# Four graph-attention layers on one core: gather every source tile but the first by index list

## The chip, the cores and the metric

The kernel runs on one core of a Trainium2 chip. The metric is the device time of one execution in microseconds, from the first to the last instruction of the program on that core. Of the engines, PE is TensorE, DVE is VectorE, ACT is ScalarE, POOL is GpSimd and SP is the sync engine, which issues most plain transfers.

## The reference

4096 nodes with 256 features pass through four attention layers. All layers use the same 4096 x 4096 adjacency matrix, which is random and sparse: the chance of an edge between i and j falls with both indices, so low-numbered nodes have many neighbours and high-numbered ones few. Cut to what matters:

```
for each layer:
    h = relu(layernorm(x))
    g = h @ W;  e = leaky_relu(src(g)[:, None] + dst(g)[None, :], 0.2)
    x = x + act(softmax(where(adj > 0, e, -inf), axis=1) @ g)
```

Layer 0 has a bias, layer 1 an ELU at its end, layer 2 four heads of 64 features. Layer 3 takes two softmaxes, one of e and one of -e, each multiplied with a projected part of 256 features, and an ELU.

## The kernel before

Nodes are cut into NT = 32 tiles of P = 128. A unit of work computes the outputs of some target tiles; it takes its sources one step at a time. In a step, DVE makes a block of unnormalised weights `s_p` out of the target's row exponentials `s_grow`, the source's scalars and the 0/1 mask (line 1019; in layer 2 ACT makes two of the four heads, line 1005, and DVE masks them, line 1028). PE then multiplies the block with the source's features and accumulates in PSUM (`s_acc`, line 1055, for layers 0, 1 and 3; `s_accm`, line 1080, for layer 2). A column of the product holds the softmax denominator.

There are two kinds of unit. A **dense unit** serves four target tiles, a block of IB = 512 columns, and steps through all 32 source tiles. Dense units serve the first 4, 2, 1 and 1 blocks of layers 0 to 3 (`DENSE`). In layers 1 to 3 their features and masks stream from DRAM in chunks of CH = 4 tiles, `s_gs` and `s_ms`, through three buffers each; in layer 0 they lie in SBUF.

A **listed unit** serves one target tile T. Here the source rows that have any edge to the tile's 128 targets are found once, in layer 0, and packed. `CAPS[T]` is the number of groups of 128 rows that the list may fill. The features of each group are fetched by an indirect DMA from the layer's `table` in DRAM (`s_gg`, line 1215, issued by POOL, nine buffers), and the mask bytes of those rows by another into `mlist` (line 915). For target blocks 1, 2 and 3 the mask bytes ride along with a feature row once (`MASKS_IN`), and ACT copies them out into `mlist` (line 1227).

The first DP = 4 source tiles are not listed. Since nearly every row there has an edge to any tile, a listed unit takes them whole, from `pre` (`g` in layer 0) and `mpre`, which stay in SBUF. So a listed unit has 4 + `CAPS[T]` steps. In layers 1 to 3 the dense units take these four tiles from SBUF too.

Lists are made in `list_sources` for each block of four target tiles, over the JT = NT - DP tiles that are listed. A reduction over the mask marks which rows are used (`seen`, line 1316), prefix sums give each row its place, and one-hot matrices `first` (line 878) and `val` (lines 865 and 869) are multiplied on PE (`idx_ps`, line 887, one matmul per source tile) to give the row numbers `idx`.

The order of work is written out by hand in a plan of steps. In layer 0, one or two listed steps follow every dense step from step 40 on (`LISTED0`), and the chunks of the adjacency matrix of blocks 4 to 7 are loaded and turned into masks on the side. In layers 1 to 3 some dense steps run alone, and the rest are spread over the listed tiles: two per tile in layer 1, 48 over 28 tiles in layer 3. A step's gather is issued six steps ahead of its matmul. Two side queues, `posts` (layer ends and the projection for the next layer) and `lists_q`, advance by a fixed number of items per step; `gather_masks` advances by `rates[2]` gathers after every dense step of layer 0. Gathers of layers 1 to 3 need the whole layer's `table`.

The order of tiles in layer 1 is 16 to 31, then 8 to 15; in layers 2 and 3 it is 8 to 31, then 4 to 7.

Of the kernel before, what the change touches and what calls it, by code (L numbers as in the profile page):

```python
# [9 lines left out]
F16 = mybir.dt.float16  # L10
U8 = mybir.dt.uint8
I32 = mybir.dt.int32
# [5 lines left out]
P = 128  # L18
N = 4096
D = 256  # L20
NT = N // P
# [431 lines left out]

DP = CH
JT = NT - DP
TS0 = IT
DENSE = (4, 2, 1, 1)

ORDER = (None, (0, 4, 1, 5, 2, 6, 3, 7), (0, 4, 5, 6, 7, 2, 1, 3), (0, 2, 3, 4, 5, 6, 7, 1))
LISTED0 = 40
CAPS = (25, 17, 15, 13, 12, 11, 11, 10, 10, 9, 9, 9, 8, 8, 8, 8) + (8,) + (7,) * 7 + (6,) * 8
MAXCAP = max(CAPS[TS0:])
OFFS = [sum(CAPS[TS0:T]) for T in range(NT + 1)]
NLIST = OFFS[NT]
# [13 lines left out]
def list_layers(ctx: ExitStack, tc: tile.TileContext, a: dict, out: bass.AP, flag):  # L480
# [305 lines left out]

    def list_constants(pool):

        place = pool.tile([P, P, JT // 2], F16, name="place")
        nc.gpsimd.iota(  # L790
            place, pattern=[[1, P], [0, JT // 2]], base=0, channel_multiplier=0, allow_small_or_imprecise_dtypes=True
        )
        lists = pool.tile([P, MAXCAP, JT * IT], F16, name="lists")
        nc.gpsimd.iota(
            lists,
            pattern=[[1, MAXCAP], [0, JT * IT]],
            base=0,
            channel_multiplier=0,
            allow_small_or_imprecise_dtypes=True,
        )  # L800

        code = pool.tile([P, JT * IT], F16, name="code")
        n = (NT // 2 - DP) * IT
        for part, tiles, base in ((code[:, 0:n], NT // 2 - DP, DP * P - HALF), (code[:, n:], NT // 2, 1)):
            nc.gpsimd.iota(
                part,
                pattern=[[CH * P, tiles // CH], [1, CH], [0, IT]],
                base=base,
                channel_multiplier=CH,
                allow_small_or_imprecise_dtypes=True,  # L810
            )
        sums = []
        for k in range(2):
            t = pool.tile([P, NT // 2 + JT, IT], F32, name=f"sums_{k}")
            nc.gpsimd.memset(t[:, 0 : NT // 2, :], 0.0)
            sums.append(t)
        return place, lists, code, sums

    def list_sources(ib, seen, pool, consts):

        n = JT * IT
        place, lists, code, sums = consts
        half = JT // 2
# [38 lines left out]
        nc.vector.tensor_copy(hib, low[:, 1].rearrange("p j t -> p (j t)"))  # L862
        yield
        val = pool.tile([P, MAXCAP, n], F16, name=f"val_{ib}", tag="val")
        nc.vector.tensor_tensor(
            val, lists, hib.unsqueeze(1).to_broadcast([P, MAXCAP, n]), op=ALU.is_equal
        )
        yield
        nc.vector.tensor_tensor(val, val, code.unsqueeze(1).to_broadcast([P, MAXCAP, n]), op=ALU.mult)
        yield  # L870
        for t in range(IT):
            T = ib * IT + t
            cap = CAPS[T]
            ps = None
            for j in range(JT):
                if j % half == 0:
                    first = pool.tile([P, P, half], F16, name=f"first_{T}_{j}", tag="first")
                    nc.vector.tensor_tensor(  # L878
                        first,
                        place,  # L880
                        lof[:, t, j : j + half].unsqueeze(1).to_broadcast([P, P, half]),
                        op=ALU.is_equal,
                    )
                    yield
                if ps is None:
                    ps = ps_mm.tile([P, MAXCAP], F32, name=f"idx_ps_{T}", tag="mm")
                nc.tensor.matmul(  # L887
                    ps[:, 0:cap],
                    lhsT=first[:, :, j % half],
                    rhs=val[:, 0:cap, j * IT + t],  # L890
                    start=(j == 0),
                    stop=(j == JT - 1),
                )
# [284 lines left out]
    def run(plan):  # L1178

        n = len(plan)  # L1180
        for p in range(n + LEAD[3]):
# [5 lines left out]
            if p >= LEAD[3]:  # L1187
                u = plan[p - LEAD[3]][0]
                clock[0] += u.cost
                pump(posts, u.rates[0], width=2)  # L1190
                pump(lists_q, u.rates[1])
                gather_masks(u.rates[2])


    def listed_sources(L, T, pool):
# [36 lines left out]
    with ExitStack() as phase:  # L1232
# [65 lines left out]
        def mask_chunk(ib, c):  # L1298

            load()  # L1300
            if ib == 0:
                behind(c)
            m = (
                mpre[:, :, ib * IB : (ib + 1) * IB]
                if c == 0
                else mpool.tile([P, CH, IB], U8, name=f"s_m_{ib}_{c}", tag="m")
            )
            for h, raw in enumerate(loaded[ib, c]):
                nc.vector.tensor_scalar(m[:, h * half : (h + 1) * half, :], raw, 0.0, None, op0=ALU.is_gt)  # L1309
            if c > 0 or ib in MASKS_IN:  # L1310
                nc.sync.dma_start(mask_rows(ib, c * CH), m)
            if ib > 0:
                if c == 0:
                    seen[ib] = lists_p.tile([P, JT, IT], F32, name=f"seen_{ib}", tag="seen", bufs=4)
                else:
                    nc.vector.tensor_reduce(
                        seen[ib][:, (c - 1) * CH : c * CH, :].rearrange("p j t -> p (j t)"),
                        m.rearrange("p j i -> p (j i)")
                        .bitcast(I32)
                        .rearrange("p (t w) -> p t w", w=P // 4),  # L1320
                        AX.X,
                        ALU.max,
                    )
# [73 lines left out]
    for l in (1, 2, 3):  # L1397
        L = layers[l]

        def all_sources(L, T0, nt, heads, per):  # L1400


            held = {}
            n = L.part
            cols = slice(heads[0] * n, (heads[-1] + 1) * n)
            w = slice(T0 * P, (T0 + nt) * P)

            def get(i):
                jt, k = divmod(i, per)
                jt = ORDER[L.l][jt // CH] * CH + jt % CH  # L1410
                mine = heads[k : k + 1] if per > 1 else heads
                if jt < DP:
                    ensure(lambda: L.ready[jt])
                    return mine, [L.pre[:, jt, h * n : (h + 1) * n] for h in mine], mpre[:, jt, w]
                if jt % CH == 0 and k == 0:
                    ensure(lambda: all(L.ready[jt : jt + CH]))
                    gt = stream.tile(
# [112 lines left out]
```

## Time and profile before

| | |
|---|---|
| device time, median of 3 runs | 1825.72 us (1823.74 to 1826.13) |
| span of the profiled execution | 1803.2 us |
| PE busy | 1658.8 us (92%) |
| DVE busy | 1322.1 us (73%) |
| ACT busy | 634.4 us (35%) |
| POOL busy | 949.8 us (53%), of it feature gathers 748.7 us (715) and mask gathers 119.4 us (105) |
| DMA | 274.70 MB, 152 GB/s on average |
| layer 0 / 1 / 2 / 3 | 0 to 545 / 545 to 855 / 855 to 1375 / 1375 to 1803 us |

A share of busy time is a mean over stages with different limits, so it is read by stage. PE's busy time comes from records whose ends are modelled, and each float32 matmul stands in the page as two records. [...]

### The profile page before, as it was taken

The page shows a single profiled execution, that of the slowest core. Times are in us where ns is not written, and L with a number is a line of the kernel's source. Part 1 is how long each engine was busy: PE and PEld are TensorE (multiplying, and loading weights), DVE is VectorE, ACT ScalarE, POOL GpSimd, SP SyncE. Part 2 cuts the span into 40 slices and gives each one's busy share as a digit, 9 for nine tenths or more (in the row PEclk, how much of TensorE's full clock was granted, in tenths as well). Part 3 has the DMA queues.
Part 4 walks back from the last instruction along what each step waited for, and adds up shares of the span by engine and source line. Part 5 has one row for each costly group of instructions (what it writes and reads, how often), then busy time and mean ns, then how long its engine had stood idle before and what let it go on. Part 6 is the DMA issues. An engine that isn't in the chain of part 4 may idle for free.

```text
span 1803.2 us, 29164 instructions
## 1 busy us (share of the span) xinstructions
PE 1658.8 (92%) x9268; PEld 1384.2 (77%) x9268; DVE 1322.1 (73%) x3908; ACT 634.4 (35%) x1915; POOL 949.8 (53%) x930
## 2 busy tenths in 40 slices
PE   6988978889899999978999999988889999999987
PEld 5876767778778778757577777788888888888876
DVE  6877867878665667645898989887786576777755
ACT  5531012001031223233376767788894011111101
POOL 9664633745642665664165353444461666554453
PEclk9998878989989999999999999999999999999999
DMA  8888757956335444544233323333342666656554
GB/s 268 277 269 278 239 162 204 289 159 179 80 80 177 125 139 124 154 136 128 71 99 86 96 79 93 94 87 85 94 121 78 194 199 188 179 168 178 169 148 122
DMA packets 152238, 274.70 MB, mean 152 GB/s; under 512 B 21424, under 2 KB 75341, under 8 KB 152077
## 3 DMA queue, kind: packets, MB, share of 16 engines
q0 software_dynamic: 45584, 130.39, 27.1%
q1 hardware_dynamic: 105656, 141.83, 24.6%
q8 instruction: 77, 1.26, 0.3%
q14 instruction: 85, 0.69, 0.1%
q10 hardware_dynamic: 836, 0.53, 0.1%
HBM read 231.76 MB, written 40.90 MB: 151 GB/s over the span
## 4 chain that ended last, share of the span: by engine, by line
PE 71%; DVE 8%; DMA 7%; issue 5%; ACT 3%; POOL 3%; another core or an unknown queue 1%; SPq 0%; POOLq 0%; ACTq 0%; DVEq 0%
PE s_acc L1055 38%; PE s_accm L1080 21%; PE s_pj L748 6%; DMA s_raw<-in_adjT 3%; DMA s_gg<-table,idx 3%; PE idx_ps L887 2%; DVE s_p L1019 2%; PE s_sT L953 1%; PE s_tp L716 1%; DVE first L878 1%; ACT s_p L1005 1%; POOL s_z L702 1%; POOL s_gg L1215 1%; DVE s_m L1309 1%
## 5 line engine op out<-in xcount | busy, mean ns | idle before, releaser
L1215 POOL DMA_INDIRECT s_gg<-table,idx x715 | 748.7, 1047 | 764.2 <-PE s_acc L1055 298.1
L1019 DVE SCALAR_TENSOR_TENSOR s_p<-s_grow,s_gg,mlist 128x128 f32<-128x128 f32 x994 | 310.0, 348 | 140.8 <-PE s_acc L1055 70.7
L1055 PE MATMUL s_acc<-s_gg,s_p 128*128 128x257 f32 x1430 | 348.5, 387 | 8.6 <-DVE s_p L1019 6.3
L1055 PEld LDWEIGHTS s_acc<-s_gg,s_p 128*128 128x128 f32 x1430 | 269.9, 193 | 52.5 <-DVE s_p L1019 11.2
L1055 PE MATMUL s_acc<-g,s_p 128*128 128x257 f32 x1152 | 298.7, 404 | 8.0 <-DVE s_p L1019 7.7
L1055 PEld LDWEIGHTS s_acc<-g,s_p 128*128 128x128 f32 x1152 | 226.8, 203 | 42.6 <-DVE s_p L1019 10.4
L1019 DVE SCALAR_TENSOR_TENSOR s_p<-s_grow,pre,mpre 128x128 f32<-128x128 f32 (+1 forms) x576 | 190.1, 370 | 46.0 <-PE s_acc L1055 35.0
L1080 PE MATMUL s_accm<-s_p,s_gg 128*65 128x128 f32 x1744 | 204.5, 273 | 1.8 <-issue 1.8
L1055 PE MATMUL s_acc<-s_gs,s_p 128*128 128x257 f32 x896 | 205.4, 383 | 0.0
L1080 PEld LDWEIGHTS s_accm<-s_p,s_gg 128*65 128x65 f32 x1744 | 193.4, 138 | 5.3 <-issue 2.8
L1005 ACT ACTIVATE s_p<-s_grow,s_minus,s_gg 128x128 f32<-128x128 f32 x436 | 187.1, 485 | 27.1 <-PE s_accm L1080 17.8
L1019 DVE SCALAR_TENSOR_TENSOR s_p<-s_grow,s_gs,s_ms 128x512 f32<-128x512 f32 x224 | 162.3, 751 | 42.9 <-PE s_accm L1080 19.9
L1055 PE MATMUL s_acc<-pre,s_p 128*128 128x257 f32 x768 | 183.7, 383 | 7.8 <-issue 3.7
L1055 PEld LDWEIGHTS s_acc<-s_gs,s_p 128*128 128x128 f32 x896 | 170.5, 191 | 25.7 <-DVE s_p L1019 1.3
L748 PE MATMUL s_pj<-s_w,s_hT 128*128 128x259 f32 (+3 forms) x640 | 171.6, 410 | 12.7 <-ACT s_g L783 3.9
L959 ACT ACTIVATE s_grow<-s_sT 128x256 f32<-128x256 f32 (+2 forms) x136 | 46.8, 368 | 344.3 <-PE s_sT L953 227.7
L1055 PEld LDWEIGHTS s_acc<-pre,s_p 128*128 128x128 f32 x768 | 143.4, 192 | 31.3 <-issue 5.2
L748 PEld LDWEIGHTS s_pj<-s_w,s_hT 128*128 128x128 f32 x640 | 125.6, 204 | 39.5 <-issue 5.2
L915 POOL DMA_INDIRECT mlist<-mask_t,idx x105 | 119.4, 1138 | 43.1 <-issue 28.9
L1080 PE MATMUL s_accm<-s_p,pre 128*65 128x128 f32 (+1 forms) x928 | 120.5, 284 | 2.0 <-issue 1.9
L1080 PEld LDWEIGHTS s_accm<-s_p,pre 128*65 128x65 f32 x928 | 103.7, 138 | 19.3 <-issue 16.5
L1005 ACT ACTIVATE s_p<-s_grow,s_minus,pre 128x128 f32<-128x128 f32 x224 | 96.2, 487 | 19.3 <-issue 15.1
(126 smaller groups left out, 1741.8 us busy)
## 6 DMA issues: line engine op xcount, KB each, us to landing
s_raw<-in_adjT SPq DMA_DIRECT2D x128, 512.0 KB
s_gs<-table SPq DMA_DIRECT2D x28, 516.0 KB
s_gg<-table,idx POOLq DMA_INDIRECT x715
mask_t<-s_m SPq DMA_DIRECT2D x35, 256.0 KB
table<-s_g SPq DMA_DIRECT2D x28, 258.0 KB
s_ms<-mask_t SPq DMA_DIRECT2D x28, 256.0 KB
table<-s_m SPq DMA_DIRECT2D x21, 256.0 KB
table<-g SPq DMA_DIRECT2D x8, 516.0 KB
```

Source lines behind the costliest of these rows:

```text
L702: (nc.gpsimd if L.l == 0 else nc.vector).tensor_scalar(z, x[:, T, :], mv[:, k, 0:1], 0.0, op0=ALU.subtract, op1=ALU.max)
L716: nc.tensor.transpose(tp[:, c, :], zs[k][:, c * P : (c + 1) * P], ident)
L748: nc.tensor.matmul(ps, lhsT=hT[:, c, :], rhs=L.w[:, c, k * (D + 6) : k * (D + 6) + cols], start=(c == 0), stop=(c == 1),)
L878: nc.vector.tensor_tensor(first, place, lof[:, t, j : j + half].unsqueeze(1).to_broadcast([P, P, half]), op=ALU.is_equal,)
L887: nc.tensor.matmul(ps[:, 0:cap], lhsT=first[:, :, j % half], rhs=val[:, 0:cap, j * IT + t], start=(j == 0), stop=(j == JT - 1),)
L915: nc.gpsimd.indirect_dma_start(out=mlist[:, OFFS[T] + k, :], out_offset=None, in_=mask_t[T // IT], in_offset=bass.IndirectOffsetOnAxis(ap= ...
L959: nc.scalar.activation(grow[:, h1:h2, :], ps[:, h1 - h0 : h2 - h0].rearrange("p h a b -> p h (a b)"), AF.Exp, scale=scale,)
L1005: nc.scalar.activation(w[:, h, :], u.grow[:, h, :], AF.Relu, scale=g[h][:, n - 1 : n], bias=minus)
L1019: nc.vector.scalar_tensor_tensor(p[:, k, :], u.grow[:, h, :], g[k][:, n - 1 : n], m, op0=ALU.min if L.l == 3 and h == 1 else ALU.max, op1= ...
L1055: nc.tensor.matmul(u.accs[it][h], lhsT=p[:, k, it * P : (it + 1) * P], rhs=g[k][:, 0:n], start=first, stop=last,)
L1080: nc.tensor.matmul(u.regions[h], lhsT=g[k][:, 0 : DH + 1], rhs=p[:, k, :],  start=first and (u.nt > 1 or h == 0), stop=last, skip_group_ch ...
L1215: nc.gpsimd.indirect_dma_start(out=wide, out_offset=None, in_=L.table, in_offset=bass.IndirectOffsetOnAxis(ap=index[T][:, k : k + 1], axis=0),
```

## The change

DP becomes 1: only the first tile of 128 sources stays whole in SBUF, and tiles 1 to 3 are listed with the others, so that rows there without an edge to the target tile are no longer multiplied. The lists grow (`CAPS`), and JT becomes 31. Summed over the listed tiles of a layer:

| layer | listed tiles | steps before | steps after | gathers before | gathers after |
|---|---|---|---|---|---|
| 0 | 16 | 169 | 144 | 105 | 128 |
| 1 | 24 | 270 | 235 | 174 | 211 |
| 2 | 28 | 330 | 291 | 218 | 263 |
| 3 | 28 | 330 | 291 | 218 | 263 |

Mask gathers grow from 105 to 128, and ACT's copies of mask bytes from 113 to 135. The dense units of layers 1 to 3 read chunk 0 from DRAM like all others, so there are 40 loads of `s_gs` and of `s_ms` for 35. The masks of chunk 0 are written to DRAM for all eight blocks, where three were before, and seven copies put the mask of tile 0 into `mpre`. `first` takes 16 or 15 tiles at a time (`HALFT`) where it took 14. In layer 0, `gather_masks` takes five masks in four dense steps where it took four.

```diff
-DP = CH
+DP = 1
 JT = NT - DP
+HALFT = (JT + 1) // 2
...
-CAPS = (25, 17, 15, 13, 12, 11, 11, 10, 10, 9, 9, 9, 8, 8, 8, 8) + (8,) + (7,) * 7 + (6,) * 8
+CAPS = (28, 20, 17, 16, 14, 13, 13, 12, 12, 11, 11) + (10,) * 4 + (9,) * 5 + (8,) * 8 + (7,) * 4
...
-                if j % half == 0:
-                    first = pool.tile([P, P, half], F16, name=f"first_{T}_{j}", tag="first")
+                if j % HALFT == 0:
+                    n = min(HALFT, JT - j)
+                    first = pool.tile([P, P, HALFT], F16, name=f"first_{T}_{j}", tag="first")
                     nc.vector.tensor_tensor(
-                        first,
-                        place,
-                        lof[:, t, j : j + half].unsqueeze(1).to_broadcast([P, P, half]),
+                        first[:, :, 0:n],
+                        place[:, :, 0:n],
+                        lof[:, t, j : j + n].unsqueeze(1).to_broadcast([P, P, n]),
...
-                gather_masks(u.rates[2])
+                gather_masks(u.rates[2] and u.rates[2] + (plan[p - LEAD[3]][1] % 4 == 3))
...
-            m = (
-                mpre[:, :, ib * IB : (ib + 1) * IB]
-                if c == 0
-                else mpool.tile([P, CH, IB], U8, name=f"s_m_{ib}_{c}", tag="m")
-            )
+            m = mpool.tile([P, CH, IB], U8, name=f"s_m_{ib}_{c}", tag="m")
...
-            if c > 0 or ib in MASKS_IN:
-                nc.sync.dma_start(mask_rows(ib, c * CH), m)
+            nc.sync.dma_start(mask_rows(ib, c * CH), m)
...
+                    nc.scalar.copy(mpre[:, :, ib * IB : (ib + 1) * IB], m[:, 0:DP, :])
...
-                if jt < DP:
-                    ensure(lambda: L.ready[jt])
-                    return mine, [L.pre[:, jt, h * n : (h + 1) * n] for h in mine], mpre[:, jt, w]
```

More of the change, by code (lines that the diff above doesn't have):

```diff
@@ L787, in list_constants @@
     def list_constants(pool):
-        place = pool.tile([P, P, JT // 2], F16, name="place")
+        place = pool.tile([P, P, HALFT], F16, name="place")
         nc.gpsimd.iota(
-            place, pattern=[[1, P], [0, JT // 2]], base=0, channel_multiplier=0, allow_small_or_imprecise_dtypes=True
+            place, pattern=[[1, P], [0, HALFT]], base=0, channel_multiplier=0, allow_small_or_imprecise_dtypes=True
         )
@@ L802, in list_constants @@
         code = pool.tile([P, JT * IT], F16, name="code")
-        n = (NT // 2 - DP) * IT
-        for part, tiles, base in ((code[:, 0:n], NT // 2 - DP, DP * P - HALF), (code[:, n:], NT // 2, 1)):
+        n1, n2 = (CH - DP) * IT, (NT // 2 - DP) * IT
+        for part, chunks, tiles, base in (
+            (code[:, 0:n1], 1, CH - DP, DP - HALF),
+            (code[:, n1:n2], NT // 2 // CH - 1, CH, CH * P - HALF),
+            (code[:, n2:], NT // 2 // CH, CH, 1),
+        ):
             nc.gpsimd.iota(
                 part,
-                pattern=[[CH * P, tiles // CH], [1, CH], [0, IT]],
+                pattern=[[CH * P, chunks], [1, tiles], [0, IT]],
                 base=base,
@@ L822, in list_sources @@
         place, lists, code, sums = consts
-        half = JT // 2
         used = pool.tile([P, JT, IT], F16, name=f"used_{ib}", tag="used")
@@ L888, in list_sources @@
                     ps[:, 0:cap],
-                    lhsT=first[:, :, j % half],
+                    lhsT=first[:, :, j % HALFT],
                     rhs=val[:, 0:cap, j * IT + t],
@@ L1314, in mask_chunk @@
                     seen[ib] = lists_p.tile([P, JT, IT], F32, name=f"seen_{ib}", tag="seen", bufs=4)
[L1315 to L1323, printed above, removed]
+                    nc.scalar.copy(mpre[:, :, ib * IB : (ib + 1) * IB], m[:, 0:DP, :])
+                j0 = DP if c == 0 else 0
+                nc.vector.tensor_reduce(
+                    seen[ib][:, c * CH + j0 - DP : (c + 1) * CH - DP, :].rearrange("p j t -> p (j t)"),
+                    m[:, j0:, :]
+                    .rearrange("p j i -> p (j i)")
+                    .bitcast(I32)
+                    .rearrange("p (t w) -> p t w", w=P // 4),
+                    AX.X,
+                    ALU.max,
+                )
                 if c == NCH - 1:
@@ L1405, in all_sources @@
             cols = slice(heads[0] * n, (heads[-1] + 1) * n)
-            w = slice(T0 * P, (T0 + nt) * P)
             def get(i):
```

## The prediction

> **What bounds the kernel now.** I read the windows view first, cut at the layer borders, which show in the chain of waits where `s_acc` gives way to `s_accm` and back.
>
> ```profile
> core 0: us, PE busy (x) PEld busy (x) DVE busy (x) ACT busy (x) POOL busy (x), PEclk, DMA share, GB/s
> 140.00:545.00 405.00, 353.35 (x1988) 293.71 (x1987) 305.81 (x794) 54.16 (x197) 213.33 (x192) 0.89 0.62 183
> 545.00:733.00 188.00, 179.12 (x839) 150.82 (x838) 120.57 (x374) 43.66 (x154) 107.32 (x105) 0.99 0.50 142
> 733.00:855.00 122.00, 101.42 (x440) 83.70 (x439) 65.67 (x202) 38.74 (x139) 68.35 (x70) 0.92 0.48 138
> 855.00:1153.00 298.00, 296.67 (x1876) 219.49 (x1875) 266.30 (x775) 192.04 (x506) 131.76 (x119) 1.00 0.33 87
> 1153.00:1375.00 222.00, 199.73 (x1622) 185.59 (x1621) 176.97 (x624) 188.56 (x550) 100.81 (x99) 0.99 0.35 96
> 1375.00:1803.00 428.00, 411.18 (x1911) 354.95 (x1909) 280.88 (x889) 52.86 (x139) 225.63 (x218) 0.99 0.57 167
> ```
>
> The rows are: layer 0 once it has lists, layer 1 in two parts, layer 2 in two parts, layer 3. PE is full in the first part of layer 2 (296.67 of 298) and nearly so in layer 3 (411 of 428). In the second part of layer 2 nobody is full: PE 0.90, ACT 0.85, DVE 0.80, each waiting for the others. In the second part of layer 1 PE falls to 0.83.
>
> Second, the groups of instructions by line, for prices.
>
> ```profile
> L1215 POOL DMA_INDIRECT s_gg<-table,idx x715 | 748.7, 1047 | 764.2 <-PE s_acc L1055 298.1
> L1019 DVE SCALAR_TENSOR_TENSOR s_p<-s_grow,s_gg,mlist 128x128 f32<-128x128 f32 x994 | 310.0, 348 | 140.8 <-PE s_acc L1055 70.7
> L1055 PE MATMUL s_acc<-s_gg,s_p 128*128 128x257 f32 x1430 | 348.5, 387 | 8.6 <-DVE s_p L1019 6.3
> L1005 ACT ACTIVATE s_p<-s_grow,s_minus,s_gg 128x128 f32<-128x128 f32 x436 | 187.1, 485 | 27.1 <-PE s_accm L1080 17.8
> L915 POOL DMA_INDIRECT mlist<-mask_t,idx x105 | 119.4, 1138 | 43.1 <-issue 28.9
> ```
>
> Each matmul stands there as two records that overlap (1430 for 715), so its price is read from the chain, in an undisturbed run of layer 3:
>
> ```profile
> 1538.95 12.15 PE s_acc L1055 x56
> ```
>
> 56 records are 28 matmuls in 12.15 us: 0.434 us each. A listed step therefore costs PE 0.434 us in layers 0 and 1 (one matmul) and 0.868 in layer 3 (two). Layer 2 has four of half that length, 0.873 (`10.45 x84` there is 42 matmuls; with 128-wide ones alone, `2.62 x24` is 12, 0.218 each).
>
> Third, POOL's timeline in the second part of layer 1, where it gets no rest:
>
> ```profile
> 801.01 0.94 POOL L1215 DMA_INDIRECT s_gg<-table,idx  x1 [0.30 <-issue]
> 802.25 0.94 POOL L1215 DMA_INDIRECT s_gg<-table,idx  x1 [0.30 <-issue]
> 803.50 1.05 POOL L1215 DMA_INDIRECT s_gg<-table,idx  x1 [0.30 <-issue]
> 804.85 0.94 POOL L1215 DMA_INDIRECT s_gg<-table,idx  x1 [0.30 <-issue]
> ```
>
> The reader is to see the 0.30 us between gathers with nothing to wait for. Busy time leaves it out. Back to back a gather takes 1.25 us, and with the mean duration of layers 1 and 3 (1.01 and 1.035 us) 1.31 to 1.34. I use 1.31. That is more than PE's 0.868 for the step it feeds.
>
> [...]
>
> **The change, part by part.** A tile of targets has CAPS+4 sources before and CAPS+1 after. [...] So 138 steps go and 150 gathers come, with 23 more mask gathers in layer 0.
>
> Layer 2, first part (tiles 8 to 21, PE full): 19 steps fewer by 0.873 = -16.6. Second part (tiles 22 to 31 and 4 to 7): 20 fewer. A step takes ACT two activations, 2 x 0.486 = 0.97, DVE two products of 0.347 and one of 0.42 = 1.11, PE 0.873; all three are nearly full, so I take 1.05 each: -21. Against it: 8 more mask copies on ACT (0.29 each, 2.3), and POOL. A tile of 8 gathers needs 8 x 1.31 = 10.5 us there against about 12.4 of the tile (13.6 before, less one step), close enough to expose some gathers: +2. Dense chunk 0 now starts after a load: +2. Sum -31.
>
> Layer 3: 39 x 0.868 = -33.9 if PE stays the limit. Per tile PE has (c+1) x 0.868 + 0.55 for target rows + 48/28 dense steps x 1.736 = 2.98; POOL has c x 1.31. At c=7: 10.5 against 9.2; c=8: 11.3/10.5; c=9: 12.2/11.8; c=10: 13.1/13.1; c=11: 13.9/14.4; c=12: 14.8/15.7; c=13: 15.7/17.0; c=14: 16.6/18.3. The larger of each, over the 28 tiles, sums to 358 against 351 for PE alone and 385 before: -27. Nine gather buffers smooth only partly, and a tile now opens with one step from SBUF in place of four, so I give back 6: -21. DMA: 45 gathers of 264 KB in some 25 us less raises the share from 0.57 to about 0.7, below the 0.98 that layer 0 reached at 316 GB/s.
>
> Layer 1: PE per tile (c+1) x 0.434 + 3.47 (two dense steps) + 3.4 (projection of layer 2 and stalls: 310 us less 228 of matmuls over 24 tiles). Tiles 16 to 31, c 9 to 7: 11.2 to 10.3 on PE, 11.8 to 9.2 on POOL: sum 175 against 183 before, -8; I count -5. Tiles 8 to 15, c 12 to 9: POOL leads, 15.7 + 2x14.4 + 4x13.1 + 11.8 = 109 against 99 before. Measured before is 122, because ACT queues behind gathers: the copy that keeps a gathered mask (line 1227) waits for the landing, and behind it stand projection and row exponentials, for which PE waits. 14 more of these copies: I take +13. Start: the first four dense steps came from SBUF; now DVE waits for 516 KB, issued at 543.8 before and used at 550, against 546.4 for the first product: +3. Sum +11.
>
> Layer 0: PE 25 x 0.434 = -10.9, and 28 tiles x 3 more index matmuls x 0.068 (14 in 0.95 us) = +5.7. DVE -25 x 0.35, `first` 56 at 2048 or 1920 elements for 1792: +5.5 at the same rate[...]. `val` 29% larger: +3.4; seven more reductions: +3.5. POOL: 46 more by 1.35 = 62 on 213 + 190 x 0.30 = 270 of 405 us, 0.82: hidden on average, in bursts not. Five more 256 KB mask writes at 280 GB/s: 4.6 us of DMA, beside DMA-heavy work. The seven copies of tile 0's mask sit on ACT, 0.13 busy there. I take +3.
>
> Sum: +3 +11 -31 -21 = -38, so 1825.7 - 38 = 1788.
>
> **Rivals.**
> - A, POOL stays hidden. For it: POOL's average is 53% and 298 us of its waits are for PE. Then layer 0 -5, layer 1 -15, layer 2 -38, layer 3 -34: -92, 1734. Against: the 0.30 us gap, and layer 1's second part as it is.
> - B, POOL, or the landing of gathers, takes PE's place everywhere, slower than before. For it: 1.31 against 0.868. Layer 1 +30, layer 0 +25[...], layer 3 -5 if transfers slow gathers by 10%, layer 2 -22: +28, 1854. Against: dense steps, 3 us in each tile of layers 1 and 3, give POOL time to catch up.
> - C, gains and give-backs cancel: layer 3 -12, layer 2 -25, layers 0 and 1 +37: 1826.
>
> **How the numbers follow.** Forecast 0.66, A 0.12, B 0.16, C 0.06. The range reaches half way towards A and into C: 1758 to 1830. It leaves out the pure forms of A and most of B. Faster is the forecast, A and a little less where the forecast comes out poor: 0.77; same 0.05; slower 0.18.
>
> **What would show it.** In the profile after, L1215 has 865 gathers at about 1.05 us. Layer 3's span is 400 to 412 us with POOL at 0.65 to 0.7 busy; layer 2 takes about 490; layer 1 310 to 330, its second part longer than 122; layer 0 ends between 535 and 560. `first` shows 1.15 to 1.25 us[...]. The forecast is wrong if PE idles on gathers in layer 3 for more than 20 us, or if layer 2's second part loses less than 10 us.

## The result and the profile after

| | before | after |
|---|---|---|
| device time, median | 1825.93 us (1823.74 to 1833.26) | 1906.70 us (1900.23 to 1911.03) |
| ratio, 95% interval | | 1.0425 (1.0379 to 1.0471) |
| span of the profiled execution | 1803.2 us | 1898.5 us |
| mean granted PE clock | 0.963 | 0.919 |
| matmul records of PE, and their busy time | 9268, 1658.8 us | 8764, 1653.4 us |

The change makes the kernel slower by 4.2%, where 1788 us (2% faster) had been forecast.

One thing about these numbers has to be known for all that follows. The runs were made in six groups, each on one chip with the kernel before beside it. The kernel before took 1826, 1808, 1804 and 1806 us in four groups and 1727 and 1730 us in two. The ratio of the change differs with it: 1.042 in the three groups of the first kind that hold the change, 1.019 in the one of the second kind that does. I call the first kind late groups and the second prompt groups, for a reason that the last section gives. Compare ratios, and stages within one kind.

The profiled execution of the kernel before was also about 20 us shorter than the timed ones of its group. So the stages of the two profiles below differ by 95 us in sum, where the measured times differ by 81.

The windows view of the kernel after, cut at the same stages as before. Columns: time, then busy us (and instructions) of PE, weight loads, DVE, ACT and POOL, then granted clock, DMA share and GB/s.

```profile
140.00:591.00 451.00, 376.64 (x2033) 304.35 (x2031) 319.09 (x790) 55.33 (x196) 271.91 (x242) 0.82 0.60 178
591.00:806.00 215.00, 185.54 (x810) 153.38 (x811) 115.86 (x346) 43.43 (x156) 126.19 (x128) 0.92 0.49 140
806.00:941.00 135.00, 103.38 (x395) 81.17 (x394) 62.83 (x190) 43.97 (x159) 82.71 (x84) 0.85 0.49 142
941.00:1240.00 299.00, 291.03 (x1758) 207.33 (x1757) 255.74 (x732) 180.08 (x478) 157.99 (x144) 1.00 0.36 98
1240.00:1455.00 215.00, 182.56 (x1413) 171.48 (x1411) 156.87 (x544) 170.12 (x505) 117.57 (x119) 0.94 0.41 116
1455.00:1898.00 443.00, 397.90 (x1777) 331.61 (x1776) 257.92 (x819) 53.99 (x143) 261.94 (x263) 0.96 0.64 192
```

Layer 0 ends at 591 us where it was 545, layer 1 is 40 us longer (27 and 13 in its parts), layer 2 is 6 shorter and layer 3 is 15 longer. In layer 3 PE has 134 records fewer than the 1911 before and loses only 13 us of busy time, while its idle time goes from 17 to 45 us. In layer 1 it is busy 8 us longer than before with 74 records fewer: the clock column fell there from 0.99 and 0.92 to 0.92 and 0.85, and in layer 0 from 0.89 to 0.82.

The groups of instructions by line, after. The second field holds total busy time and the mean ns of one; the third is the engine's idle time before them, with what ended it.

```profile
L1220 POOL DMA_INDIRECT s_gg<-table,idx x865 | 890.6, 1030 | 679.5 <-PE s_acc L1060 173.3 <-issue 142.5 <-PE s_accm L1085 126.1
L1024 DVE SCALAR_TENSOR_TENSOR s_p<-s_grow,s_gg,mlist 128x128 f32<-128x128 f32 x1204 | 380.3, 346 | 276.9 <-DMA s_gg<-table,idx 148.5 <-PE s_acc L1060 80.6 <-PE s_accm L1085 15.9
L883 DVE TENSOR_TENSOR first<-place,lof 128x2048 f16<-128x2048 f16 x28 | 35.9, 1283 | 0.0
L883 DVE TENSOR_TENSOR first<-place,lof 128x1920 f16<-128x1920 f16 x28 | 35.4, 1263 | 45.8 <-remote 24.5 <-PE idx_ps L892 16.7 <-PE s_sT L958 3.3
```

A gather costs POOL what it cost before (a mean of 1030 ns for 1047). What changed is the second line: before the products of gathered rows DVE now sits idle for 277 us where it was 141, and for 148.5 us of it the wait ends with the landing of a gather (the end of its transfer), where it was 23.4. POOL's record of a gather ends sooner: at the median it lasts 0.947 us in the kernel before, whose chain of waits has waits of up to 5.7 us on a landing. In layer 3 alone (the view of waits, DVE, kernel before and then after; us in total, times, longest):

```profile
DVE s_p L1019 <- DMA s_gg<-table,idx: 13.2, 12, 3.0
```

```profile
DVE s_p L1024 <- DMA s_gg<-table,idx: 82.5, 72, 5.1
```

### The profile page after: what moved, and what is told of

It reads as the page before. It is cut to its first block, busy times and chain, and to the rows that moved or that the text cites. A ratio compares the mean times of both kernels' runs of the same rounds, so it can differ in the third digit from the quotient of the medians.

```text
span 1898.5 us, 28296 instructions
## 1 busy us (share of the span) xinstructions
PE 1653.4 (87%) x8764; PEld 1344.8 (71%) x8764; DVE 1272.2 (67%) x3660; ACT 612.5 (32%) x1866; POOL 1119.7 (59%) x1104
## 5 line engine op out<-in xcount | busy, mean ns | idle before, releaser
L1220 POOL DMA_INDIRECT s_gg<-table,idx x865 | 890.6, 1030 | 679.5 <-PE s_acc L1060 173.3
L1024 DVE SCALAR_TENSOR_TENSOR s_p<-s_grow,s_gg,mlist 128x128 f32<-128x128 f32 x1204 | 380.3, 346 | 276.9 <-DMA s_gg<-table,idx 148.5
L1060 PE MATMUL s_acc<-s_gg,s_p 128*128 128x257 f32 x1730 | 447.3, 403 | 29.7 <-DMA s_gg<-table,idx 11.2
L1060 PEld LDWEIGHTS s_acc<-s_gg,s_p 128*128 128x128 f32 x1730 | 341.2, 203 | 93.7 <-issue 27.4
L1085 PE MATMUL s_accm<-s_p,s_gg 128*65 128x128 f32 x2104 | 256.8, 277 | 5.8 <-issue 4.8
L1060 PEld LDWEIGHTS s_acc<-g,s_p 128*128 128x128 f32 x1056 | 215.8, 211 | 45.1 <-DVE s_p L1024 10.5
L1085 PEld LDWEIGHTS s_accm<-s_p,s_gg 128*65 128x65 f32 x2104 | 239.4, 141 | 11.7 <-issue 5.6
L1085 PE MATMUL s_accm<-s_p,s_gs 128*65 128x512 f32 x256 | 115.9, 592 | 0.0
L1024 DVE SCALAR_TENSOR_TENSOR s_p<-s_grow,g,s_m 128x512 f32<-128x512 f32 x128 | 98.0, 772 | 13.3 <-remote 5.5
L883 DVE TENSOR_TENSOR first<-place,lof 128x2048 f16<-128x2048 f16 (+1 forms) x56 | 71.3, 1273 | 45.8 <-remote 24.5
L1310 DVE TENSOR_SCALAR s_m<-s_raw 128x1024 uint8<-128x1024 int32 x128 | 90.6, 719 | 16.4 <-DMA s_raw<-in_adjT 14.1
L892 PEld LDWEIGHTS <-first 128*128 128x128 f16 x868 | 62.3, 164 | 51.9 <-DVE first L883 25.5
```

What stands on the lines that cost most here:

```text
L883: nc.vector.tensor_tensor(first[:, :, 0:n], place[:, :, 0:n], lof[:, t, j : j + n].unsqueeze(1).to_broadcast([P, P, n]), op=ALU.is_equal,)
L892: nc.tensor.matmul(ps[:, 0:cap], lhsT=first[:, :, j % HALFT], rhs=val[:, 0:cap, j * IT + t], start=(j == 0), stop=(j == JT - 1),)
L1024: nc.vector.scalar_tensor_tensor(p[:, k, :], u.grow[:, h, :], g[k][:, n - 1 : n], m, op0=ALU.min if L.l == 3 and h == 1 else ALU.max, op1= ...
L1060: nc.tensor.matmul(u.accs[it][h], lhsT=p[:, k, it * P : (it + 1) * P], rhs=g[k][:, 0:n], start=first, stop=last,)
L1085: nc.tensor.matmul(u.regions[h], lhsT=g[k][:, 0 : DH + 1], rhs=p[:, k, :],  start=first and (u.nt > 1 or h == 0), stop=last, skip_group_ch ...
L1220: nc.gpsimd.indirect_dma_start(out=wide, out_offset=None, in_=L.table, in_offset=bass.IndirectOffsetOnAxis(ap=index[T][:, k : k + 1], axis=0),
```

## The experiments

Two theories stood first. **G**: the 37 to 45 more gathers in each of layers 1 to 3 are what costs. **R**: the dense part of the change costs (the masks' new way through layer 0, and dense blocks that read chunk 0 from the table). The change was taken apart along that line.

**The dense part alone** (the lists as before, four tiles whole in SBUF):

```
- DP = 1                      + DP = CH     (lists and listed steps as before)
  CAPS = those of the kernel before
  dense blocks read chunk 0 from the table; every chunk 0 is written to HBM; ACT copies it to mpre
```

> The changed kernel with DP back at 4 and the old CAPS: steps and gathers as before, but dense units read chunk 0 from the table, chunk 0's masks are written for all blocks, and ACT copies them to mpre. If the surplus gathers cost the time (G), this part is small: within 10 us of before, 1816 to 1836. If the other parts of the change cost it (R: loads of chunk 0, ACT waiting for the mask, more DMA), most of the 81 us stays: 1865 or more.

Measured: 1755.29 us, 1.0170 (1.0132 to 1.0208), prompt group. It came out between the two theories. In two things this kernel isn't the change's dense part alone, and both lie in layer 0. Its seven copies to `mpre` hold four tiles (1.90 us each) where the change copies one (0.62 us). And it has the change's faster order of mask gathers, five in four dense steps, but only the 105 gathers of before. What came of the second is told with the chain of three kernels below.

**The shorter tiles without the surplus gathers** (the steps of the kernel after; 715 + 105 gathers instead of 865 + 128):

```
-            if i < DP:
+            if i < DP or i - DP >= CB[T]:        # CB: CAPS of the kernel before
                 the step takes tile 0 from SBUF, no gather
```

> The changed kernel, lists, steps and dense part unaltered, but in each listed unit the last CAPS(after) - CAPS(before) steps use the tile in SBUF again in place of a gathered group (their sources are left out of the sum), so that 715 feature and 105 mask gathers remain. G: PE's saving comes through, 1735 to 1785. R: the time stays near the changed kernel's, 1860 or more.

Measured: 1688.42 us, 0.9775 (0.9738 to 0.9813), prompt group, as G has it. This leaves sources out, so it isn't a usable version, but it prices the two halves of the listed part. With the surplus gathers their 22 mask copies on ACT are gone too, so the two are priced together.

**Gathers that nobody reads** (the kernel before, with the 150 more gathers, of 512 bytes a row, into two spare buffers):

```
+                if k < CA[T] - CAPS[T]:
+                    spare = pool.tile([P, 128], F32, tag="gx", bufs=2)
+                    nc.gpsimd.indirect_dma_start(out=spare, ..., index[T][:, k : k + 1])
```

> The kernel before with 150 surplus gathers (512 bytes a row, into two spare buffers that nobody reads), as many in each tile as the change adds; PE, DVE and ACT do what they did. If it is POOL's issue rate that costs the time (G1), 1850 to 1900. If it is the landing of gathers that somebody waits for (G2: data used, not issue time), at most 1845. R: at most 1835.

Measured: 1769.41 us, 1.0250 (1.0211 to 1.0289), prompt group. The group of these instructions:

```profile
L1226 POOL DMA_INDIRECT s_gx<-table,idx x150 | 155.2, 1035 | 45.7 <-issue 35.0 <-DVE s_p L1020 4.0 <-DMA s_gg<-table,idx 1.5
```

No engine computes with their data, and 0.025 x 1727 = 43 us reach the end, as a ratio within the range that was expected if issuing costs (G1). Issuing them takes 155 us of POOL plus 0.30 us between gathers. They are also issued ahead of other gathers, whose packets go through the same queue (q0 on the page of this run, 140.23 MB for 130.39 before: the 9.8 MB of the 150), and the two weren't told apart. Where the 43 us fall is read below, with the windows by layer.

**Is it the number of buffers, or the order on DVE?** With 14 gather buffers for nine, and with DVE's products three steps before the matmul turned into one (`LEAD` (0, 2, 3, 6) to (0, 2, 5, 6)), so that the reciprocals that end a tile no longer stand behind products of the next tile's gathers. Both beside a fresh run of the kernel after. The two unaltered kernels were meant for the chip of the first experiments, but this group ran on another and is a late one.

> The kernel before, unaltered, for a profile from the chip of the experiments, where the kernel before took 1727 us and not 1826. Either theory: ratio 1.00; its layers should be shorter than in the first profile, the same work in less time.

> The changed kernel, unaltered, on the chip of the experiments. G (surplus gathers cost the time) and R (the other parts): the ratio is again 1.03 to 1.05, 1780 to 1815. If the ratio is nearer to 1.00 here, the loss is of a kind that depends on the chip's memory or clock, which would speak for waits on landings.

> The changed kernel with 14 gather buffers in layers 1 to 3 in place of 9. If gathers start too late for want of buffers (G2), PE's waits shrink and layers 1 and 3 lose 10 us or more each against the changed kernel. If POOL's issue rate binds (G1), nothing starts earlier: within 5 us of the changed kernel.

> The changed kernel with weights made one step ahead of the matmul and not three (LEAD 0, 2, 5, 6). With three, the products of the next tile's first gathers stand on DVE's queue ahead of the reciprocal that frees the last tile's accumulators (H). If H costs much, layer 3 loses 10 us or more against the changed kernel, its waits of PE for s_y go, and layer 1 does not gain more than 5. If G1 alone, no gain, and a loss where PE now waits for DVE.

Measured: the kernel before 0.999 (0.994 to 1.004), after 1.0417 (1.0372 to 1.0462), 14 buffers 1.0521 (1.0459 to 1.0582), the other lead 1.0604 (1.053 to 1.0679). Neither is a cure. With 14 buffers every layer of the profile is longer than in the kernel after of this group, so want of buffers isn't the main cause. The other lead is less clear: its layer 3 took 439 us where the kernel after took 446, short of the 10 us that were expected, and its loss lies in layer 2 (522 for 510) and in layer 0 (585 for 567, within the scatter given below). It also takes away the slack of two steps, so it doesn't price the queue of reciprocals alone, and that queue isn't refuted as part of the cause.

**Bytes, PE work, the ACT copy.** Again beside the kernel after; this group was a prompt one.

```
half rows:    out=wide[:, 0 : L.part] if L.l == 3 else wide          # layer 3, both heads use head 0's columns
SBUF steps:   DP + 3 + CAPS[T] steps in layers 1 to 3, the 3 from tile 0 in SBUF
DVE copy:     nc.vector.tensor_copy(mpre[...], m[:, 0:DP, :])        # was nc.scalar.copy, line 1315
```

> The changed kernel as it is, as the yardstick for the runs beside it. Chips differ (the kernel before took 1726.9, 1808.5 and 1825.9 us on three of them), and the run with fewer gathers was made on the fastest. If the loss is in the kernel alone, the ratio to the kernel before is 1.035 to 1.05 again. If part of it comes from the chip (on the two slower ones PE's semaphore updates come late, in batches), the ratio is nearer 1.02 on a chip where they do not.

> Leaves out: in layer 3 each gather fetches only the 258 columns of head 0 (half the bytes, same number of gathers), and both heads use them. If the bytes or the landing of a gather set layer 3's pace, layer 3 falls from 443 us by 20 us or more. If what counts is the number of gathers, each 1.25 us of POOL plus its waits, layer 3 stays within 8 us of the changed kernel beside it, and so does the total.

> Adds work that counts twice: in layers 1 to 3 every listed tile opens with three more steps from the SBUF tile (84 steps a layer: 36 us of PE in layer 1, 73 in layer 2, 73 in layer 3 at full clock), as the kernel before had them; the gathers stay. If gathers set the pace of layers 1 and 3, these steps fill time in which PE waited: layer 1 grows by 0 to 12 us, layer 3 by 0 to 15, layer 2 (PE full) by 55 to 75. If PE work plus fixed waits make up the time, layer 1 grows by 36 and layer 3 by 65 to 75.

> The copy of the first tile's mask (line 1315, seven of them in layer 0) runs on DVE in place of ACT. ACT waited 26.8 us there for the mask that DVE writes, up to 12.7 at once, with row exponentials and projection queued behind. If that wait is on the path, layer 0 shortens by 10 to 25 us against the changed kernel; if it lies beside other waits, by under 5.

Measured: the kernel after 1.0194 (1.0149 to 1.0239); half rows 1.0121 (1.008 to 1.0161), layer 3 from 411 to 402 us; SBUF steps 1.0891 (1.0845 to 1.0937), layer 1 +16, layer 2 +54, layer 3 +53 us; DVE copy 1.0197 (1.0146 to 1.0247). In the half rows both heads take one head's features, so the outputs of layer 3 are wrong and only the time counts. Bytes are a small part: halving them gives 9 us in layer 3 (one profile of each), between the two expectations. Of the 182 us of PE work that the SBUF steps add, 0.0697 x 1729.5 = 121 come out as time: layer 1 hides more than half of it, layers 2 and 3 about a quarter. Layer 3 fell between the two expectations, far above the 15 us of "gathers set the pace", so in a prompt group layer 3 is paced by PE for the most part even after the change. Which engine makes the small copy doesn't matter.

**The two halves once more, on a late group**, and the kernel before for its stages:

> The kernel before as it is, for its stages on this chip. If its trace shows PE's semaphore updates late and in batches (48 and 50 pauses in the two earlier profiles of it), the time is near 1810 to 1826 us; if not, near 1727, with layer 1 near 285 us, layer 2 near 500, layer 3 near 415 to 420.

> The changed kernel as it is, as the yardstick beside the others. With late PE updates in the trace: ratio 1.035 to 1.05 to the kernel before. Without: 1.015 to 1.025.

> The dense part of the change alone, as in the first run of it (ratio 1.017 where PE's updates came on time). If this part costs loads, mask writes and copies only, the ratio is 1.012 to 1.022 on any chip; if late PE updates weigh on it as on the whole change, 1.03 or more on such a chip.

> Leaves out the surplus gathers (their steps take the SBUF tile instead, so those sources are missing), as in the first run of it (ratio 0.9775 where PE's updates came on time). If the gathers are what late PE updates hurt, the ratio on a chip with late updates is again 0.97 to 0.985, so that the gathers' share of the loss grows there from 4 to 6 or 7 points; if late updates hurt the shorter tiles as such, it is near 1.0 there.

Measured: before 0.9995 (0.9968 to 1.0022), after 1.0426 (1.0381 to 1.0471), dense part alone 1.0220 (1.0183 to 1.0256), fewer gathers 0.9949 (0.9922 to 0.9977). The last is what was expected if a late group hurts the shorter tiles as such, and the surplus gathers cost more there too. The windows by layer, first of the prompt groups: dense part alone, fewer gathers, kernel after.

```profile
0.00:537.00 537.00, 479.44 (x2603) 395.19 (x2604) 410.49 (x1052) 133.38 (x442) 314.39 (x320) 0.92 0.70 215
537.00:830.00 293.00, 273.59 (x1259) 232.08 (x1259) 186.67 (x571) 79.32 (x287) 173.71 (x174) 0.96 0.52 149
830.00:1327.00 497.00, 491.69 (x3469) 403.56 (x3468) 438.50 (x1393) 380.64 (x1055) 235.52 (x218) 0.99 0.35 96
1327.00:1750.00 423.00, 411.63 (x1942) 358.17 (x1940) 290.24 (x895) 53.45 (x140) 219.79 (x218) 0.99 0.59 173
```

```profile
0.00:542.00 542.00, 473.02 (x2619) 388.89 (x2619) 419.64 (x1033) 120.26 (x428) 319.64 (x321) 0.91 0.68 212
542.00:826.00 284.00, 259.56 (x1205) 220.88 (x1206) 175.10 (x535) 83.27 (x301) 172.88 (x174) 0.96 0.53 156
826.00:1294.00 468.00, 456.55 (x3146) 367.42 (x3145) 405.26 (x1274) 347.31 (x976) 236.95 (x218) 1.00 0.36 102
1294.00:1690.00 396.00, 380.63 (x1799) 329.73 (x1797) 265.86 (x820) 53.75 (x141) 224.00 (x218) 0.99 0.63 185
```

```profile
0.00:546.00 546.00, 476.55 (x2619) 393.37 (x2620) 420.68 (x1034) 120.42 (x428) 371.66 (x367) 0.90 0.71 217
546.00:857.00 311.00, 269.86 (x1206) 222.27 (x1205) 177.89 (x536) 86.77 (x314) 208.25 (x211) 0.96 0.55 158
857.00:1350.00 493.00, 467.99 (x3170) 376.82 (x3169) 409.69 (x1276) 352.40 (x984) 278.63 (x263) 0.98 0.40 110
1350.00:1761.00 411.00, 383.44 (x1775) 326.80 (x1773) 256.35 (x817) 53.43 (x141) 266.51 (x263) 0.99 0.69 207
```

Read down one layer. Layer 2 goes 497, 468, 493: the shorter tiles give 29 us, the gathers take 25 back. Layer 3 goes 423, 396, 411, layer 1 293, 284, 311. The last count in brackets is POOL's: 37 to 45 gathers more. In layer 2 POOL is only 0.57 busy with them (278.63 of 493; about 0.73 with the 0.30 us between gathers), and they still cost 25 us. Differences of such windows, in us, for both kinds of group:

| | layer 0 | layer 1 | layer 2 | layer 3 |
|---|---|---|---|---|
| shorter tiles, prompt | +5 | -9 | -29 | -27 |
| shorter tiles, late | -20 | -2 | -31 | -17 |
| surplus gathers, prompt | +4 | +27 | +25 | +15 |
| surplus gathers, late | -6 | +44 | +16 | +31 |

(Each is from one profile of each kernel; in both rows on surplus gathers the kernel after is from another group of the same kind than the one with fewer gathers. Layer 0 scatters between profiles of one kernel: in late groups the kernel after ended it at 567, 591 and 593.)

The gathers that nobody reads, in layers 1 to 3, prompt group:

```profile
524.00:835.00 311.00, 278.82 (x1261) 233.23 (x1260) 184.55 (x569) 80.14 (x290) 208.01 (x211) 0.94 0.51 143
835.00:1341.00 506.00, 493.58 (x3471) 406.01 (x3470) 440.14 (x1394) 381.22 (x1055) 283.13 (x263) 0.99 0.37 99
1341.00:1767.00 426.00, 412.81 (x1941) 357.53 (x1939) 287.16 (x894) 53.20 (x140) 263.48 (x263) 0.99 0.59 175
```

Beside the dense part alone, which has as many steps and the gathers of before, they cost 18 us in layer 1, 9 in layer 2 and 3 in layer 3. (A few us more in all, perhaps, since the dense part alone reads chunk 0 from the table, which took 4.5 us when it was tried by itself.) The surplus gathers of the change cost 27, 25 and 15. So a gather costs without a reader, in layer 1 above all, but in layers 2 and 3 most of the price comes only where its data are used and tiles are short. (The tiles of the kernel with unread gathers are the long ones of before.) Where that shows in layer 2 are ACT's waits for landings, for a gathered row and for a gathered mask, with fewer gathers and then in the kernel after (an edit above them shifts the lines by one):

```profile
ACT s_p L1011 <- DMA s_gg<-table,idx: 6.0, 6, 3.0
ACT mlist L1233 <- DMA s_gg<-table,idx: 5.8, 7, 2.1
```

```profile
ACT s_p L1010 <- DMA s_gg<-table,idx: 18.7, 23, 2.6
ACT mlist L1232 <- DMA s_gg<-table,idx: 12.2, 16, 2.1
```

PE in turn waits 9 us there for ACT's other results (`s_hT`, `s_g`, `s_o`) with fewer gathers and 20 us with all. In layer 3 it is the end of a tile that holds PE up: it waits for ACT to read the accumulators (`s_y`), which needs a reciprocal on DVE, and DVE's products wait for landings (34.6 us with fewer gathers, 97.1 with all). PE's wait, in the same two kernels:

```profile
PE s_acc L1061 <- ACT s_y L1172: 0.6, 2, 0.4
```

```profile
PE s_acc L1060 <- ACT s_y L1171: 12.4, 8, 3.5
```

These 12 us are most of the 15 that the surplus gathers cost in layer 3. That one wait passes on to the next is read from the traces; no run broke the chain.

**What in the dense part costs**: a chain of three kernels in which each adds a piece to the one ahead, late group, on the chip that had been prompt.

```
reads:   before, and dense blocks of layers 1 to 3 take chunk 0 from the table (one more mask write)
writes:  the same, and dma_start(mask_rows(ib, c * CH), m) for all blocks, as in the change
rest:    the same, and chunk 0's mask goes through a pool tile and nc.scalar.copy to mpre,
         and gather_masks takes one more after every fourth dense step   (= the dense part alone)
```

> The kernel before, with only the dense blocks of layers 1 to 3 reading their first chunk from the table instead of SBUF (and the one mask write that this needs). The prediction had put this at 2 to 5 us (3 in layer 1, 2 in layer 2). If it is the dense part's cost, ratio 1.01 or more; if as predicted, 1.000 to 1.004.

> The same, and the mask rows of chunk 0 are written to HBM for all blocks (four more writes of 256 KB in layer 0). If the writes load the transfers of layer 0, the ratio is 0.005 above the run beside it or more, and layer 0 is 10 us longer; if they are hidden, within 0.003 of it.

> The whole dense part again (1.017 and 1.022 before): over the run beside it, chunk 0's mask goes through a pool tile and an ACT copy in listed and dense blocks alike, and one more mask gather is issued after every fourth dense step. If these are the cost, the ratio is 1.015 to 1.025 while the two beside it are under 1.007, and the gap is in layer 0's dense stretch.

Measured: reads 1.0025 (1.0001 to 1.0050), writes 1.0017 (0.9993 to 1.0042), rest 1.0197 (1.0157 to 1.0237). Layer 0 with the writes, and then of the dense part alone in the other late group:

```profile
0.00:544.00 544.00, 472.44 (x2602) 389.58 (x2603) 412.27 (x1051) 119.91 (x433) 321.05 (x320) 0.92 0.68 212
```

```profile
0.00:593.00 593.00, 496.69 (x2605) 404.73 (x2605) 410.71 (x1052) 134.57 (x447) 311.15 (x320) 0.88 0.63 195
```

The same matmuls take PE 24 us more, at a clock of 0.88 for 0.92, and it idles 25 us more. (The first profile lies 6 us below the median of its runs and the second 11 above.) So nearly all of this kernel's loss is the rest: the way of chunk 0's mask through layer 0 and the earlier mask gathers, which were not separated. But it can't be handed to the change as it stands. POOL's waits at the mask gathers for row numbers that aren't made yet, in layer 0 from 140 us on, of the dense part alone and of the kernel after (late groups):

```profile
POOL mlist L919 <- DVE idx L901: 76.6, 3, 31.1
```

```profile
POOL mlist L920 <- DVE idx L902: 3.8, 1, 3.8
```

In the kernel with the writes it is 11.7 us, in two waits. With 105 mask gathers and the faster order, POOL comes to a tile before its list is ready, stands there three times for 20 to 31 us, and the feature gathers of layer 0 stand behind. The change, with 128 gathers in the same order, has no such wait; the kernel with fewer gathers has it again (77.5 us prompt, 78.7 late). So the 33 us of the rest price a stall of the experiment's own and copies four times as large along with what the change does. What the change itself loses in layer 0 is the difference of whole kernels: 20 to 46 us in late groups (567 to 593 us, where the kernel before ended it at 545 and 547). In the prompt groups it ended at 546, and the kernel before with the unread gathers at 524. The copy's engine isn't to blame, since the DVE copy gave the same time in the whole change. Which part is, stays open.

No run that computes everything beat the kernel before.

## Why the prediction was wrong

Ratios of the runs multiplied with the time of the kernel before in their group:

| part | predicted, us | prompt groups | late group |
|---|---|---|---|
| dense part, with the stall of its kernel | +5, and nothing for its copies and mask gathers | +29 (1.0170) | +40 (1.0220) |
| shorter tiles, longer lists, gathers as before | -84 | -68 (to 0.9775) | -49 (to 0.9949) |
| surplus gathers | +40 | +72 (to 1.0194) | +86 (to 1.0426) |
| sum | -39 (-38 as forecast, unrounded) | +33 | +77 |

The predicted column sorts the prediction's terms. Shorter tiles are -98 (11, 15, 38 and 34 in layers 0 to 3), and the longer lists of layer 0 give 14 back. The gathers are 13 in layer 3 (34 less 21), 4 in layer 2 and 23 in layer 1 (15 of PE work that became +8). The stall that two of the kernels have in layer 0 doesn't touch the sums, but it shifts time of layer 0 between the rows. Layers 1 to 3 are free of it.

- **PE work per step: right.** By the steps' prices (25 and 35 at 0.434, 39 at 0.873, 39 at 0.868), less 6 us of index matmuls, 88 us of PE work were to go. PE's busy time fell by 1656.4 - 1569.8 = 87 us from the dense part alone to fewer gathers. Of this, 68 us of time followed in a prompt group and 49 in a late one. (That nearly every row of the first tiles has an edge to any tile holds for low targets only: over the 28 tiles of layer 3, 45 more groups of 128 rows do for 84 tiles that were taken whole.)
- **The price of the surplus gathers, the first failed step.** The prediction charged a gather where POOL's time for a tile exceeds PE's, and little where it doesn't. It failed most in layer 2: "A tile of 8 gathers needs 8 x 1.31 = 10.5 us there against about 12.4 of the tile ... close enough to expose some gathers: +2." The surplus gathers took 25 us there (16 in late groups). Over layers 1 to 3 they took 67 us in prompt groups (27, 25 and 15) and 91 in late ones (44, 16 and 31), where 40 were forecast (23, 4 and 13). The comparison of two steady rates says nothing of gathers that come later than the engine in front of them can use. What the runs show in its place: gathers that nobody reads cost 30 us in layers 1 to 3 by issue and transfer alone, and with readers the landing waits of DVE and ACT grow and pass on to PE. The prediction's own mark for being wrong, under 10 us lost in layer 2's second part, was met: 222 us became 215.
- **Layer 1: one number right by luck.** The forecast had -2 for its first part (-5, and +3 at the start) and +13 for its second; the profiles give +27 (188 to 215) and +13 (122 to 135). The reason given for the +13 did not come about: ACT's wait for landings before the mask copy was to grow, and in the second part it is 60.0 us in 53 waits, as before (62.4 in 53). DVE waits instead. In the prompt groups its wait for landings in layer 1 is 38.3 us with fewer gathers and 79.4 with all, and PE's wait for its products 1.6 and 15.9.
- **Layer 3: the form was right in prompt groups.** 13 us were forecast for the gathers, and 15 measured there; 31 in late ones. The other mark, PE idle on gathers for over 20 us, was met only in part: PE idles 28 us more than before, but 15.3 us of its waits end with ACT's `s_y` (1.8 before) and 2.7 with a landing or with DVE's product.
- **Layer 0, the second failed step.** "The seven copies of tile 0's mask sit on ACT, 0.13 busy there. I take +3." The +3 is for the whole layer, and it lost 20 to 46 us in late groups. The table reads and the mask writes were priced rightly (5 us forecast for the reads, 0.0025 x 1806 = 4.5 measured, with an interval from 0 to 9; nothing for the writes). What else the layer loses isn't shown, for the reasons above: the mask's new way, the lists and the 46 more gathers remain. That a low busy share of ACT was taken for free room was a step without a reason, but no run shows that this step is what cost.
- **The clock, left out of the sum.** Every matmul was priced at full clock. The share of clock not granted, over the span, was 1803.2 x 0.037 = 67 us before and 1898.5 x 0.081 = 154 after. These 87 us are about what is missing: 88 us of PE work were to go, and PE is only 5 us less busy (1653 for 1659) with 504 records fewer. In the trace after, the granted clock is 0.5 or 1, and 38 of its 44 stretches at half clock last 3.4, 6.8 or 10.2 us (before, 15 of 19 last 3.4 or 6.8). Cut into windows of 3.41 us, the shortest stretch, in step with these stretches, 37 of the 43 at full clock in which PE was busy for under half were followed by half clock, and none of the 343 in which it was busy for 90% or more. So where PE idled for over 1.7 us of such a window, half clock mostly came next, and the idle time may cost clock as well as itself. How much of the loss that is was not tested: no run kept the stalls and took away the half clock. In prompt groups the surplus gathers add 17 us of clock not granted (84.5 for 67.6) to some 71 us of time.
- **`first` on odd rows: right in the main.** It runs at 1283 and 1263 ns for 2048 and 1920 elements against 1088 for 1792, a little over the 1.15 to 1.25 us forecast: 0.626 and 0.658 ns an element for 0.607. That the rate would stay the same was the author's estimate, for shapes that the kernel before doesn't have. The means mix two kinds, since a row of `lof` now has 31 elements of 2 bytes: the first and third target of a block start on an even element and took 1209 to 1226 ns (2048) and 1228 to 1231 (1920), the second and fourth on an odd one, with 1344 to 1355 and 1295 to 1298. That is 11% and 5% for the odd start. The price of `first` is 10 us of DVE in place of 5.5.
- **Which rival came true.** Rival B (gathers take PE's place, 1854 us) is nearest in direction, but with another account: layer 2 gained 6 us, not 22.

In the prompt group the stages of the kernel after were close to what was forecast for them: layer 1 311 us (310 to 330 forecast), layer 2 493 (490), layer 3 411 (400 to 412), end of layer 0 546 (535 to 560). That is luck: there the kernel before takes 1730 us and not 1826, and the gain had been reckoned from the stages of a late group.

## What to carry to other kernels

Comparing mean rates per tile (POOL's 1.3 us against PE's 0.87 with dense work between) finds the bound of a steady stream and not the price of one more transfer in a queue. Price an added gather by two runs, one with transfers that nobody reads and one with the real ones, since the first gave 30 us here where the second gave 67. And before a part of a change is priced by a kernel that holds this part alone, look in its trace for a wait that neither whole kernel has: here the dense part alone brought 70 us of waits on POOL of its own.

## What was not expected of the hardware

**PE's semaphore updates can come late, in batches.** The trace holds the times at which semaphores were updated. In the kernel after, layer 3, in its profile from the late group of the 14 buffers: PE starts 16 records without a pause, and DVE and POOL, which wait for its buffers, start at the times below (the timeline of PE, of DVE and of POOL).

```profile
1515.90 3.64 PE L1060 MATMUL s_acc<-s_gg,s_p 128*128 128x257 f32 x16
```

```profile
1517.00 0.61 DVE L1024 SCALAR_TENSOR_TENSOR s_p<-s_grow,s_gg,mlist 128x128 f32<-128x128 f32 x2 [0.77 <-PE s_acc L1060]
1518.44 0.62 DVE L1024 SCALAR_TENSOR_TENSOR s_p<-s_grow,s_gg,mlist 128x128 f32<-128x128 f32 x2 [0.82 <-PE s_acc L1060]
```

```profile
1516.49 0.95 POOL L1220 DMA_INDIRECT s_gg<-table,idx  x1 [0.30 <-issue]
1518.73 0.94 POOL L1220 DMA_INDIRECT s_gg<-table,idx  x1 [1.29 <-PE s_acc L1060]
```

```
updates of PE's semaphore, us: 1514.66  1516.98  1517.02  1518.42  1518.47  1518.52  1518.58  1518.64  1518.68
```

The matmul records start 0.217 us apart, yet between 1517.02 and 1518.42 there is no update, and then six come 0.04 to 0.06 us apart. DVE starts 0.02 us after the first of each batch. The trace doesn't say what holds the updates back.

Counting pauses of over 0.5 us that end in three or more updates under 0.06 us apart: the kernel before has 48, 50 and 50 in its three late profiles, the kernel after 59, 64 and 48. The seven kernels profiled in prompt groups have none, whatever they do. In the first profile of each kernel, 32 of the 48 pauses before and 29 of the 59 after are within 0.06 us of 0.72 us or of two to four times that. One chip was prompt in one group and late in another, so it isn't the chip alone.

Two cautions. The late traces hold fewer of these records, 2063 to 2078 updates of PE's semaphore for the kernel after where the prompt trace has 2491, so a pause can in part be records that are missing; and what the view of waits says of late groups is rougher for it. That DVE and POOL start with the batches speaks for pauses that are real.

Late groups are 4 to 6% slower for the kernel before and 7 to 8% for the kernel after, and the change costs twice as much in them. Slower transfers don't seem to be the reason: in the dense part alone the packets of the gathers' queue took 27.8% of 1750.2 = 487 us in the prompt group and 25.6% of 1858.0 = 476 in the late one. That the late updates make the difference is likely, since DVE and POOL are seen to start on them, but nothing here could switch them off, and what brings them on stays open.

**The surplus gathers do not cost mainly by bytes**: with half the bytes in layer 3 only 9 of its 411 us went. The time from issue to landing was not varied.
